# Two graph attention layers on one core: the norm's sums on ScalarE, the own-row product as a bf16 map, the scores of layer 1 after the second gather, and a new order of the start

## The chip, the cores and the metric

The kernel runs on one core of one Trainium2 chip. The metric is the device time of one execution in microseconds, as a median over runs. A profile of one further execution gives every instruction's start and length. PE is TensorE, DVE is VectorE, ACT is ScalarE, POOL is GpSimd, and SP issues the DMAs.

## The reference, cut to what matters

```python
# x: (16, 1024, 64) f32; adj: (16, 1024, 1024) int32, about 9 ones in a row, symmetric, ones on the diagonal
# layer 0: 8 heads of 64, edge kinds adj
q, k, v = x @ Wq + bq, x @ Wk + bk, x @ Wv + bv            # each reshaped to 8 heads
scores  = leaky_relu(q k^T / 8 + edge_bias[adj], 0.2)      # where adj > 0, else -1e9
x = layernorm(x + softmax(scores) v @ Wp + bp)             # over the 64 features, eps 1e-5
# layer 1: additive attention
hp = x @ lin_w^T + lin_b
u, v = hp @ W1^T, hp @ W2^T
e = sum_f a_f * leaky_relu(u_i + v_j, 0.2)                 # where adj > 0, else -9e15
x = layernorm(x + elu(softmax(e) hp))
```

## The kernel before, in words

The kernel uses the few ones of a row. Of each batch it first makes short lists of neighbours: groups of 8 rows share a list of columns. Those lists select rows of x (as one-hot matrices), and both attentions run over 120 slots per group instead of 1024 columns. A path over all pairs exists behind a flag and isn't taken with these inputs.

**Setup.** Weights are loaded and folded on PE and DVE (`aqk`, `wvp`, `wc8`, `lin2`, `w1h`, `w2d`), in tile pools that are closed before the pools of the main part open. `wc8` holds the same 512 numbers in a pattern with zeros; it is written in 128 copies of one column (L121).

**Lists of a batch** (`prepare`, `finish`). 16 pieces of adj (`ad`, 256 KB each, four buffers) are loaded; DVE turns each into 0 or a small number in bf16 (`ab`, L325, one buffer for half a batch); PE sums them with a code (`pat`, L334); DVE takes the best 40 of each segment with MAX8 and MATCH_REPLACE8 (L345 to L380), and writes the columns (`col`) and the row codes (`slot`) to DRAM, from where `cb` and `rows_s` come back copied over partitions. `prepare` is a generator of 41 pieces. Batch 0 is prepared whole at the start; a later batch is prepared in pieces, at five *places* in each step of the main loop (`lists.place(g, 0)` to `(g, 4)`), at most two pieces at a place. Small jobs (`side`) are advanced one piece at each place too.

**Main loop.** The order on every engine is the program's order, written out by hand. Step g works on tile g of layer 0 (eight tiles of 128 rows to a batch, so 128 in all) and on tile u = g - 12 of layer 1; the parts of a tile are spread over several steps. A step's main parts in their order on PE, with the lines of the profile:

- layer 0 `score` (L626), `gather` (L504, two halves), `heads` (L694), `rows`, `queries` (L605);
- layer 1 `project` of the tile before: `pz` takes the neighbours' product (L760) and the own row's product (L766). For the latter `own_rows` makes `ub`, the row of u repeated in 8 copies of which a mask leaves one (POOL, L748), and `rw`, a row of slots (ACT, L753);
- place 1; layer 1 `gather` first half (L504), `turn_weights` (L800, and its copy `eT` by DVE, L802); layer 0 `turn` (L523); place 2;
- layer 1 `weigh`, the scores from r (L786), and their maximum m (DVE, L788); `exps` (ACT, L794); layer 0 `indicate` (DVE, L480, two instructions); layer 1 `gather` second half;
- layer 0 `turn_weights` (L668, copies `w` by ACT, L670), layer 1 `turn`; place 3; layer 1 `indicate` (L480) and `own_rows`; layer 0 `attend` (z, L678), layer 1 `attend` (L811); place 4.

Between `project` and `weigh` stands r: ACT takes the positive part (L771) and DVE adds the rest (L772). The PSUM tag "e" has one bank; it is used in turn for `back`, for the transposed weights (L800, read by `eT`) and for the scores of `weigh`.

The norm (`Norm`) takes two tiles at once: DVE makes mean and variance with bn_stats and bn_aggr (L550, L551); POOL adds eps, takes the power -0.5 (L559), subtracts and multiplies (L558 to L563). Layer 0 does this in `residual`, layer 1 in `end`.

Of the kernel before, what the change touches and what calls it, by code (L numbers as in the profile page):

```python
# [22 lines left out]
GR = 8  # L23
# [10 lines left out]
def kernel(  # L34
# [18 lines left out]
    fst = fast.enter_context(tc.tile_pool(name="fst", bufs=1))  # L53
    setup = ExitStack()
    ps_c = setup.enter_context(tc.tile_pool(name="ps_c", bufs=4, space=bass.MemoryType.PSUM))
    tmp = setup.enter_context(tc.tile_pool(name="tmp", bufs=1))
    ident = cst.tile([P, P], F32, name="ident")
# [4 lines left out]
    nc.gpsimd.memset(ones, 1.0)  # L62


    def sub(n):
        return slice(n * D, n * D + D)

    def load_w(w, name, rows_, cols_):
        t = tmp.tile([rows_, cols_], F32, tag=name, name=name)
        nc.sync.dma_start(t, w)  # L70
        return t
# [14 lines left out]
    def head_T(w, name):  # L86
        t = tmp.tile([P, NC, D], F32, tag=name, name=name)
        for c in range(NC):
            pw = bank(f"{name}_{c}")
            nc.tensor.transpose(pw[:, 0, 0:D], w[:, ts(c, P)], ident[0:D, 0:D])  # L90
            nc.vector.tensor_copy(t[:, c, :], pw[:, 0, 0:D])
        return t
# [12 lines left out]
    qb = fst.tile([P, H], F32, name="qb")  # L105
    wc8 = halves("wc8", [GR, H, GR])
    wc1 = tmp.tile([1, H], F32, name="wc1")
    for h in range(H):
        c, r = h // 2, sub(h % 2)
        pw = bank(f"h_{h}")  # L110
        pc = bank(f"hc_{h}")
        for n in range(2):
            o = sub(n)
            nc.tensor.matmul(pw[o, 0, 0:D], wqT[r, c, :], wkT[r, c, :], start=True, stop=True)
            nc.tensor.matmul(pw[o, 1, 0:D], wvT[r, c, :], wp_l[r, c, :], start=True, stop=True)
            nc.tensor.matmul(pw[o, 2, 0:1], wkT[r, c, :], bq_c[r, c : c + 1], start=True, stop=True)
            nc.tensor.matmul(pw[o, 3, 0:1], wqT[r, c, :], bk_c[r, c : c + 1], start=True, stop=True)
            nc.vector.tensor_scalar(aqk[o, h, :], pw[o, 0, 0:D], QS1, None, ALU.mult)
            nc.vector.tensor_copy(wvp[o, h, :], pw[o, 1, 0:D])
            for i in range(GR):  # L120
                nc.vector.tensor_scalar(wc8[o, i, h, i : i + 1], pw[o, 3, 0:1], QS1, None, ALU.mult)  # L121
        nc.vector.tensor_scalar(qb[:, h : h + 1], pw[:, 2, 0:1], QS1, None, ALU.mult)
        nc.tensor.matmul(pc[0:1, 0, 0:1], bq_c[r, c : c + 1], bk_c[r, c : c + 1], start=True, stop=True)
        nc.vector.tensor_scalar(wc1[:, h : h + 1], pc[0:1, 0, 0:1], QS1, None, ALU.mult)
    eb1 = tmp.tile([1, H], F32, name="eb1")
    nc.sync.dma_start(eb1, edge_bias[1:2, :])
# [108 lines left out]
    nc.gpsimd.iota(jrow, [[-P, SEG // P]], base=SEG, channel_multiplier=-1, allow_small_or_imprecise_dtypes=True)  # L235

    bad = cst.tile([P, 1], F32, name="bad")
    nc.vector.memset(bad, 0.0)
# [19 lines left out]

    per = fast.enter_context(tc.tile_pool(name="g_per", bufs=1))
    dbl = fast.enter_context(tc.tile_pool(name="g_dbl", bufs=2))  # L260
    sml = fast.enter_context(tc.tile_pool(name="g_sml", bufs=4))
    ps_g = fast.enter_context(tc.tile_pool(name="ps_g", bufs=2, space=bass.MemoryType.PSUM))
    ps_s = fast.enter_context(tc.tile_pool(name="ps_s0", bufs=2, space=bass.MemoryType.PSUM))
    ps_p = fast.enter_context(tc.tile_pool(name="ps_p", bufs=2, space=bass.MemoryType.PSUM))
    ps_z = fast.enter_context(tc.tile_pool(name="ps_z", bufs=1, space=bass.MemoryType.PSUM))

# [42 lines left out]
    def prepare(b):  # L309
# [10 lines left out]
        for hs in range(2):  # L320
            ab = per.tile([P, NT, 2, SEG], BF16, tag="ab", name=f"ab_{b}_{hs}")
            for T in range(NT):
                ad = ads.pop(hs * NT + T)

                nc.vector.tensor_scalar(ab[:, T, :, :], ad, 1.0 - TINY, 0.0, ALU.subtract, ALU.max)  # L325
                if T % 4 // 2 == hs:
# [69 lines left out]
        for n in range(2):  # L396
            for s in range(NSEG):
                nc.sync.dma_start(col_d[:, s, n], col[sub(n), s, :])
        yield
        hv = who.rearrange("p (s a) k -> p s a k", a=2)  # L400
# [12 lines left out]
        for n in range(2):  # L413
            for q in range(NQ):
# [5 lines left out]
                )  # L420
        edges[b] = col_d
        late[b] = (flags, dg, rows_s)
# [22 lines left out]

    def thirds(src, tag, nm):

        t3 = dbl.tile([P, 3, NT, D], BF16, tag=tag, bufs=3, name=f"{tag}_{nm}")
        less = per.tile([P, NT, D], F32, tag="less", name=f"less_{tag}_{nm}")
# [91 lines left out]
    class Norm:  # L541
# [5 lines left out]

        def look(self, y, t):
            s6 = sml.tile([P, 6], F32, tag="st", name=f"st_{self.nm}_{t}")
            nc.vector.bn_stats(s6, y[:, t, :])  # L550
            nc.vector.bn_aggr(self.mv[:, t, :], s6)  # L551

        def scale(self, dst, y, t):
            two = slice(t - 1, t + 1)
            for t_ in (t - 1, t):
                self.look(y, t_)
            rs = sml.tile([P, 2], F32, tag="rs", name=f"rs_{self.nm}_{t}")
            nc.gpsimd.tensor_tensor(rs, self.mv[:, two, 1], eps.to_broadcast([P, 2]), ALU.add)  # L558
            nc.gpsimd.tensor_tensor(rs, rs, root.to_broadcast([P, 2]), ALU.pow)  # L559
            nc.gpsimd.tensor_tensor(  # L560
                dst[:, two, :], y[:, two, :], self.mv[:, two, 0:1].to_broadcast([P, 2, D]), ALU.subtract
            )
            nc.gpsimd.tensor_tensor(  # L563
                dst[:, two, :], dst[:, two, :], rs.unsqueeze(2).to_broadcast([P, 2, D]), ALU.mult
            )

    class Layer0(Tiles):
# [145 lines left out]
        def residual(self, t):  # L713
            if t % 2 == 0:
                return
            nc.vector.tensor_tensor(self.y[:, t - 1 : t + 1, :], self.pr, self.xs[:, t - 1 : t + 1, :], ALU.add)
            self.norm.scale(self.y, self.y, t)

# [8 lines left out]
    class Layer1(Tiles):  # L727
# [9 lines left out]
        def sums(self):  # L737
# [4 lines left out]
            self.u = dbl.tile([P, NT, D], F32, tag="u", bufs=1, name=f"u_{self.b}")  # L742
            nc.vector.tensor_tensor(self.u, pu, rows_b[:, 0:1, :].to_broadcast([P, NT, D]), ALU.add)

        def own_rows(self, t):
            nm = f"{self.b}_{t}"
            ub = dbl.tile([P, NQ, D], F32, tag="ub", name=f"ub_{nm}")
            nc.gpsimd.tensor_tensor(  # L748
                ub, self.u[:, t, :].unsqueeze(1).to_broadcast([P, NQ, D]), in_q.unsqueeze(2).to_broadcast([P, NQ, D]),
                ALU.mult,  # L750
            )
            rw = dbl.tile([P, SLOTS], F32, tag="rw", name=f"rw_{nm}")
            nc.scalar.activation(rw, masks[self.b][:, t, :], AF.Identity, bias=ones[:, 0:1], scale=-1.0 / NEG)  # L753
            self.rows_[t] = ub, rw

        def project(self, t):
            xg, (ub, rw) = self.xg[t], self.rows_.pop(t)
            pz = banks("s", f"pz_{self.b}_{t}")
            for n, c_ in CORNERS:
# [3 lines left out]
                )  # L763
            for p in range(4):
                for n, c_ in CORNERS:
                    nc.tensor.matmul(  # L766
                        pz[n][sub(c_), p, :], ub[sub(n), 2 * p + c_, :], rw[sub(n), :], start=False, stop=(p == 3)
                    )
# [28 lines left out]
        def turn_weights(self, t):  # L797
# [3 lines left out]
            eT = dbl.tile([SLOTS, P], F32, tag="eT", name=f"eT_{nm}")  # L801
            nc.vector.tensor_copy(eT, pt)  # L802
            self.e[t] = eT
# [25 lines left out]
        def end(self):  # L829
# [13 lines left out]
            for t in range(1, NT, 2):  # L843
                norm.scale(o, y, t)
                yield
                yield
# [17 lines left out]
    class Lists:  # L864


        def __init__(self):
# [5 lines left out]
            self.work = parts()  # L873
            self.done, self.part, self.side = 0, None, []

        def place(self, g, k):
# [3 lines left out]
            end = self.done + 2 if (t, k) != (NT - 1, PLACES - 1) else due  # L880
            while self.done < min(due, end) and self.part != ("keys" if last else "sums"):
                self.part = next(self.work, None)
                self.done += 1
            while self.side:
                if next(self.side[0], 0) is None:
                    break
                self.side.pop(0)

    order = ["PE", "Activation", "DVE", "Pool", "SP"]
    lists = Lists()  # L890
    with tc.manual_schedule(engines={getattr(mybir.EngineType, e) for e in order}):
        for _ in prepare(0):
            pass
        for _ in finish(0):
            pass
        l0[0] = Layer0(0)
        for _ in lists.side.pop():
            pass
        l0[0].constants()
        l0[0].load(0)  # L900
        l0[0].load(1)
        l0[0].indicate(0)
        l0[0].own(0)
        for g in range(NT * B + LAG + 7):
            u = g - LAG
# [27 lines left out]
            lists.place(g, 2)  # L933
            at(l1, u - 1, "weigh")
            at(l1, u - 1, "exps")
            at(l0, g + 1, "indicate")
            at(l0, g + 2, "load")
            at(l1, u, "gather", 1)
            if t == 2 and b - 1 in l0:
                x1 = l0[b - 1].end()  # L940
# [438 lines left out]
```

## Time and profile before

| | |
|---|---|
| median of 3 runs | 2493.3 us (2490.24 to 2495.37) |
| profiled execution | 2495.43 us, its span 2493.5 us |
| granted clock of TensorE | 0.98 of full speed on the mean; 0.83 in the first 200 us, 1.00 from 300 us on |
| busy: PE, DVE, ACT, POOL | 91%, 78%, 59%, 41% |
| first gather on PE | at 95.25 us |
| one batch in the steady state | 145.63 us (1138.70 to 1284.33) |

The span is from the first instruction to the last. A row of groups shows the line, the engine, the operation, tiles written and read, the count, the busy time in all and the mean length of one. A row of waits reads "who <- for whom: us in total, times, longest". A row of a timeline shows start, length, and in brackets the idle time of the engine just before and who ended it.

### The profile page before, as it was taken

The page shows a single profiled execution, that of the slowest core. Times are in us where ns is not written, and L with a number is a line of the kernel's source. Part 1 is how long each engine was busy: PE and PEld are TensorE (multiplying, and loading weights), DVE is VectorE, ACT ScalarE, POOL GpSimd, SP SyncE. Part 2 cuts the span into 40 slices and gives each one's busy share as a digit, 9 for nine tenths or more (in the row PEclk, how much of TensorE's full clock was granted, in tenths as well). Part 3 has the DMA queues.
Part 4 walks back from the last instruction along what each step waited for, and adds up shares of the span by engine and source line. Part 5 has one row for each costly group of instructions (what it writes and reads, how often), then busy time and mean ns, then how long its engine had stood idle before and what let it go on. Part 6 is the DMA issues. An engine that isn't in the chain of part 4 may idle for free.

```text
span 2493.5 us, 112320 instructions
## 1 busy us (share of the span) xinstructions
PE 2260.5 (91%) x49218; PEld 1910.4 (77%) x49218; DVE 1943.8 (78%) x5365; ACT 1459.4 (59%) x4417; POOL 1017.8 (41%) x1489
## 2 busy tenths in 40 slices
PE   5377899999999999999999999999999999999996
PEld 4266788888787887878788787878878787888864
DVE  6586878888887888788788878878887887876542
ACT  0054566666565665656566565656666665666743
POOL 1033433535354453534445353444535344443431
PEclk9688999999999999999999999999999999999998
DMA  3313242333233242323324332332423233132211
GB/s 103 96 56 119 79 146 78 108 113 119 81 97 124 78 129 92 122 78 92 129 78 127 93 121 78 96 124 78 142 85 116 78 117 104 57 100 67 70 38 29
DMA packets 192710, 239.10 MB, mean 96 GB/s; under 512 B 91732, under 2 KB 157332, under 8 KB 192212
## 3 DMA queue, kind: packets, MB, share of 16 engines
q1 hardware_dynamic: 192212, 231.85, 29.9%
q8 instruction: 388, 6.36, 1.0%
q14 instruction: 110, 0.90, 0.1%
HBM read 226.58 MB, written 5.21 MB: 93 GB/s over the span
## 4 chain that ended last, share of the span: by engine, by line
PE 62%; DVE 30%; DMA 3%; issue 3%; ACT 1%; POOL 1%; SPq 0%; POOLq 0%; ACTq 0%; DVEq 0%
PE pg L504 20%; PE pt L523 5%; PE s L626 5%; DVE r L772 4%; PE z L678 4%; PE pp L668 4%; PE pa L811 4%; PE po L694 3%; DMA ad<-in_adj_dram 3%; DVE f L480 3%; PE e L786 3%; PE pq L605 3%; DVE qp L610 2%; PE pat L334 2%; PE pz L766 2%
## 5 line engine op out<-in xcount | busy, mean ns | idle before, releaser
L504 PE MATMUL pg<-f,x 128*64 128x272 bf16 (+2 forms) x13312 | 807.1, 273 | 37.3 <-DVE f L480 33.7
L504 PEld LDWEIGHTS <-x 128*64 128x64 bf16 x13312 | 662.4, 110 | 117.5 <-issue 71.9
L660 POOL TENSOR_TENSOR ls<-ls,den 128x480 f32<-128x480 f32 x256 | 298.5, 1166 | 595.9 <-DVE den L659 593.1
L510 ACT COPY xg<-pg 128x448 f32<-128x448 f32 x512 | 271.6, 530 | 388.2 <-PE pg L504 386.3
L480 DVE TENSOR_SCALAR f<-cb,jrow 128x2176 bf16<-128x2176 bf16 x512 | 411.4, 847 | 0.1
L652 ACT ACTIVATE ls<-ls,mx 128x120 f32<-128x120 f32 x1024 | 391.3, 386 | 0.0
L524 ACT COPY xn<-pt 120x512 f32<-120x512 f32 x512 | 278.2, 598 | 43.6 <-PE pt L523 41.8
L523 PE MATMUL pt<-ident,xg 128*120 128x128 f32 x2048 | 271.6, 275 | 15.7 <-DVE qp L610 15.2
L523 PEld LDWEIGHTS pt<-ident,xg 128*120 128x120 f32 x2048 | 230.7, 138 | 23.7 <-DVE qp L610 16.7
L771 ACT ACTIVATE r<-pz 128x480 f32<-128x480 f32 x256 | 132.1, 568 | 174.5 <-PE pz L766 174.5
L489 POOL COPY xg<-xT 128x64 f32<-128x64 f32 x256 | 107.9, 432 | 291.3 <-PE pt L523 291.3
L634 DVE TENSOR_TENSOR sc<-s,rowc 128x480 f32<-128x480 f32 x256 | 155.5, 649 | 84.6 <-PE s L626 82.7
L772 DVE SCALAR_TENSOR_TENSOR r<-pz,r 128x480 f32<-128x480 f32 x256 | 155.6, 649 | 54.3 <-ACT r L771 53.2
L652 ACT ACTIVATION_READ_ACCUMULATOR ls<-ls,mx 128x1 f32 x1024 | 194.7, 190 | 0.0
L558 POOL TENSOR_TENSOR rs<-mv,eps 128x2 f32<-128x2 f32 x128 | 32.3, 253 | 359.2 <-DVE den L659 280.6
L642 DVE SCALAR_TENSOR_TENSOR ls<-sc 128x480 f32<-128x480 f32 x256 | 175.5, 686 | 0.0
L643 DVE TENSOR_REDUCE mx<-ls 128x4 f32<-128x480 f32 x256 | 167.2, 653 | 8.8
L766 PEld LDWEIGHTS pz<-rw,ub 64*64 64x64 f32 x4096 | 121.3, 133 | 62.7 <-issue 61.3
L678 PE MATMUL z<-w,xn 120*64 120x64 f32 x4096 | 158.7, 228 | 4.8 <-ACT w L670 4.1
L678 PEld LDWEIGHTS z<-w,xn 120*64 120x64 f32 x4096 | 137.6, 140 | 28.6 <-ACT w L670 26.3
L610 DVE TENSOR_TENSOR qp<-pq,qb 128x256 f32<-128x256 f32 x256 | 96.2, 418 | 78.9 <-PE pq L605 78.5
L748 POOL TENSOR_TENSOR ub<-u,in_q 128x512 f32<-128x512 f32 x128 | 155.4, 1215 | 0.1
(216 smaller groups left out, 4169.1 us busy)
## 6 DMA issues: line engine op xcount, KB each, us to landing
cb<-col_d SPq DMA_DIRECT2D x271, 544.0 KB
ad<-in_adj_dram SPq DMA_DIRECT2D x256, 256.0 KB
xs<-in_x_dram SPq DMA_DIRECT2D x32, 128.0 KB
rows_s<-slot_d SPq DMA_DIRECT2D x256, 14.0 KB
out_dram<-o SPq DMA_DIRECT2D x32, 128.0 KB
col_d<-col SPq DMA_DIRECT2D x128, 4.2 KB
dg<-in_adj_dram SPq DMA_DIRECT2D x32, 2.0 KB
slot_d<-slot SPq DMA_DIRECT2D x16, 28.0 KB
```

Of the source, the lines that this page charges most:

```text
L480: nc.vector.tensor_scalar(fj.rearrange("p s n q k -> p (s n q k)"), cb.rearrange("p s n q k -> p (s n q k)"), jrow[:, j : j + 1], None, AL ...
L504: nc.tensor.matmul(pg[sub(n), :, FIRST * a_ + lo : FIRST * a_ + to], self.t3[:, k, 4 * hs + 2 * a_ + j, :], f[j][:, 2 * hs + a_, n, :, lo:to],
L510: nc.scalar.copy(dst, pg)
L523: nc.tensor.transpose(pt[:, q, :], xg[:, 4 * m + q, :], ident)
L524: nc.scalar.copy(self.xn[t][:, ts(m, 4), :], pt)
L642: nc.vector.scalar_tensor_tensor(ls, scs[n], SLOPE, scs[n], ALU.mult, ALU.max)
L643: nc.vector.tensor_reduce(self.mx[:, n, ts_], ls, XX, ALU.max, negate=True)
L652: nc.scalar.activation(ls[:, q, :], ls[:, q, :], AF.Exp, bias=neg[:, q : q + 1], accum_out=den[:, q : q + 1])
L660: nc.gpsimd.tensor_tensor(ls, ls, den.unsqueeze(2).to_broadcast([P, 4, SLOTS]), ALU.mult)
L678: nc.tensor.matmul(zz[sub(n), q, :], xn[:, q, sub(n)], w_[n][:, q // 2, sub(q % 2)], start=True, stop=True)
L766: nc.tensor.matmul(pz[n][sub(c_), p, :], ub[sub(n), 2 * p + c_, :], rw[sub(n), :], start=False, stop=(p == 3))
L772: nc.vector.scalar_tensor_tensor(r, pz[n], SLOPE / (1.0 - SLOPE), r, ALU.mult, ALU.add)
```

## The change

- **Own row's product as a map.** `sums` splits u into three bf16 parts (`thirds`, on POOL, one piece at a place). `own_rows` makes `rw` in bf16 and from it `rq`, the row of slots in 8 copies of which a mask leaves one (POOL, 960 elements for 512 of `ub`). `project` takes 3 x 4 products of 64x64 by 480 columns in bf16 where it took 4 x 4 of 64x64 by 120 columns in f32.
- **Moved scores.** `weigh` and `exps` of layer 1 come after the second half of the gather, and so after `indicate` of layer 0 on DVE.
- **Norm.** Two ACTIVATEs with a row sum give the two means (Identity), POOL subtracts; at the next place two more (Square) give the variances, and POOL does the rest. `Norm.scale` is a generator; layer 0 puts it into a list of its own that is advanced at each place.
- **A copy.** `eT` is made by ACT.
- **Start.** The pools of the main part are opened before those of setup; `wc8` is made by one product; batch 0's `ab` is made by ACT; the first `cb` loads, `constants` and Layer0 come ahead of the row codes' loads and of `finish(0)`; at g = 0 no piece of a list is made.

```diff
@@ setup
-    wc8 = halves("wc8", [GR, H, GR])
+    wc8 = fst.tile([P, GR, H, GR], F32, name="wc8")
...
-            for i in range(GR):
-                nc.vector.tensor_scalar(wc8[o, i, h, i : i + 1], pw[o, 3, 0:1], QS1, None, ALU.mult)
+        nc.vector.tensor_scalar(wcv[:, h : h + 1], pw[:, 3, 0:1], QS1, None, ALU.mult)
...
+    nc.vector.tensor_tensor(
+        wc8, wcv.unsqueeze(1).unsqueeze(3).to_broadcast([P, GR, H, GR]),
+        same.unsqueeze(2).to_broadcast([P, GR, H, GR]), ALU.mult,
+    )
@@ prepare
-                nc.vector.tensor_scalar(ab[:, T, :, :], ad, 1.0 - TINY, 0.0, ALU.subtract, ALU.max)
+                if b:
+                    nc.vector.tensor_scalar(ab[:, T, :, :], ad, 1.0 - TINY, 0.0, ALU.subtract, ALU.max)
+                else:
+                    nc.scalar.activation(ab[:, T, :, :], ad, AF.Relu, bias=below)
...
+        edges[b] = col_d
         yield
@@ Norm
         def scale(self, dst, y, t):
-            for t_ in (t - 1, t):
-                self.look(y, t_)
...
+            for t_ in (t - 1, t):
+                nc.scalar.activation(
+                    part, y[:, t_, :], AF.Identity, scale=1.0 / D, accum_out=self.mv[:, t_, 0:1]
+                )
             nc.gpsimd.tensor_tensor(
                 dst[:, two, :], y[:, two, :], self.mv[:, two, 0:1].to_broadcast([P, 2, D]), ALU.subtract
             )
+            yield
+            for t_ in (t - 1, t):
+                nc.scalar.activation(
+                    part, dst[:, t_, :], AF.Square, scale=1.0 / D**0.5, accum_out=self.mv[:, t_, 1:2]
+                )
...
@@ Layer0.residual
-            self.norm.scale(self.y, self.y, t)
+            lists.norms.append(self.norm.scale(self.y, self.y, t))
@@ Layer1
+            self.u3, parts = thirds(self.u, "u3", f"{self.b}", 2)
+            lists.side.insert(0, parts)
...
-            ub = dbl.tile([P, NQ, D], F32, tag="ub", name=f"ub_{nm}")
...
+            rw = dbl.tile([P, SLOTS], BF16, tag="rw", name=f"rw_{nm}")
+            nc.scalar.activation(rw, masks[self.b][:, t, :], AF.Identity, bias=ones[:, 0:1], scale=-1.0 / NEG)
+            self.rows_[t] = rq = dbl.tile([P, NQ, SLOTS], BF16, tag="rq", name=f"rq_{nm}")
+            nc.gpsimd.tensor_tensor(
+                rq, rw.unsqueeze(1).to_broadcast([P, NQ, SLOTS]), in_q.unsqueeze(2).to_broadcast([P, NQ, SLOTS]), ALU.mult
+            )
...
-            for p in range(4):
+            for k in range(3):
                 for n, c_ in CORNERS:
                     nc.tensor.matmul(
-                        pz[n][sub(c_), p, :], ub[sub(n), 2 * p + c_, :], rw[sub(n), :], start=False, stop=(p == 3)
+                        pz[n][sub(c_), :, :], self.u3[sub(n), k, t, :],
+                        rq[sub(n), :, :].rearrange("p (g c) k -> p c g k", c=2)[:, c_, :, :], start=False, stop=(k == 2),
                     )
...
-            nc.vector.tensor_copy(eT, pt)
+            nc.scalar.copy(eT, pt)
@@ place
-            while self.done < min(due, end) and self.part != ("keys" if last else "sums"):
+            while g > 0 and self.done < min(due, end) and self.part != ("keys" if last else "sums"):
...
-            while self.side:
-                if next(self.side[0], 0) is None:
-                    break
-                self.side.pop(0)
+            for queue in (self.side, self.norms):
+                while queue:
+                    if next(queue[0], 0) is None:
+                        break
+                    queue.pop(0)
@@ main loop
-            at(l1, u - 1, "weigh")
-            at(l1, u - 1, "exps")
             at(l0, g + 1, "indicate")
             at(l0, g + 2, "load")
             at(l1, u, "gather", 1)
+            at(l1, u - 1, "weigh")
+            at(l1, u - 1, "exps")
```

## The prediction

> **What bounds the kernel now.** I read the busy shares first, then PE's waits, then one period of the steady state step by step, then its timeline, and last the chain before the first gather.
>
> ```profile
> PE 2260.5 (91%) x49218; PEld 1910.4 (77%) x49218; DVE 1943.8 (78%) x5365; ACT 1459.4 (59%) x4417; POOL 1017.8 (41%) x1489
> ```
>
> PE is the busiest, but 91% is a mean over a start of 95 us before the first gather and a thin end. PE's waits between 300 and 2200 us:
>
> ```profile
> PE e L786 <- DVE eT L802: 75.5, 76, 1.5
> PE pt L800 <- DVE den L659: 7.0, 20, 0.5
> ```
>
> So in the steady state PE is paced by its own order but for one wait: `weigh` (L786) writes the bank that `eT` (L802) must have left, and DVE comes late to that copy. Over the run it is 83.4 us. One batch, cut at the end of each L766 group, has eight steps of 145.63 us in all. The busy time by stretches gives the last two of them and the sums:
>
> ```profile
> 1247.44:1265.14 17.70, 16.17 (x372) 14.17 (x373) 16.79 (x58) 11.12 (x34) 5.93 (x10) 1.00 0.19 66
> 1265.14:1284.33 19.19, 17.83 (x412) 15.39 (x413) 17.79 (x46) 11.49 (x35) 8.55 (x9) 1.00 0.45 130
> sum 145.63, PE 137.64 PEld 117.17 DVE 120.29 ACT 90.81 POOL 63.91; mean PE 17.21 PEld 14.65 DVE 15.04 ACT 11.35 POOL 7.99
> ```
>
> Columns after the length: PE, PEld, DVE, ACT, POOL. In these two steps DVE idles only 0.91 and 1.40 us: there DVE sets the pace, in the other six PE does. PE's timeline of one step:
>
> ```profile
> 1207.74 0.99 PE L760 MATMUL pz<-xg,w2d 64*64 64x480 f32 x8
> 1208.55 1.00 PE L766 MATMUL pz<-rw,ub 64*64 64x120 f32 x32
> 1209.48 1.59 PE L504 MATMUL pg<-f,x 128*64 128x272 bf16 x26
> 1211.16 1.04 PE L523 MATMUL pt<-ident,xg 128*120 128x128 f32 x8
> 1213.72 0.62 PE L786 MATMUL e<-r,a_two 128*32 128x120 f32 x16 [1.53 <-DVE eT L802]
> 1214.32 1.59 PE L504 MATMUL pg<-f,x 128*64 128x272 bf16 x26
> 1217.79 1.48 PE L678 MATMUL z<-w,xn 120*64 120x64 f32 x31
> ```
>
> **The product with u (L766).** From its start to the next group's it takes 1209.48 - 1208.55 = 0.93 us. In its place come 12 bf16 products of 64x64 by 480 columns. The rate: L504's 26 products of 272 columns take 1.52 us, two column halves beside each other, so 0.117 us a pair or 0.43 ns a column; 480 columns are 0.206 us. L760 has four corners beside each other (8 records of 567 ns within 0.81 us). Four at a time, 12 products are 3 rounds, 0.62 us: a gain of 0.31 us. Two at a time it would be 1.24 us, a loss of 0.31. I take four at a time, because L760 is the same shape. 128 x 0.31 = 40 us of PE; in the two DVE-paced steps of eight it does not arrive, so 30 us (ends: +40 and -40).
>
> **weigh after the second gather, and eT on ACT.** Call P the end of the product with u. Today DVE does r (to P+1.87), then the work of two places, and eT in the middle of it; that is the 1.53 us. In the new order weigh stands behind 1.52 us more of PE work, and eT stands in ACT's queue behind one xg copy, about P+2.6. The wait on L786 goes. What is late next: `exps` now stands in ACT directly ahead of the two w copies, and waits for the maximum m (L788), which in DVE now stands behind both L480 of the next tile:
>
> ```profile
> 1215.99 0.25 DVE L788 TENSOR_REDUCE m<-e 128x1 f32<-128x120 f32 x1
> 1216.16 1.47 DVE L480 TENSOR_SCALAR f<-cb,jrow 128x2176 bf16<-128x2176 bf16 x2
> ```
>
> z (L678) needs both w. From m's start to the end of the second w is 0.28 + 0.05 + 0.45 + 1.08 = 1.86 us (DVE row, hop, exp with its read, two L670 copies). PE's own order gives z at P + 1.52 + 0.16 + 0.95 + 1.52 + 0.67 + 0.95 + 0.95, about P+6.66 (first gather, L800, L523, second gather, weigh, L668, L523). So z waits where m starts later than P+4.8. m's place is r's end, plus both places' DVE work, plus 1.42 for the L480 pair. In the step above (P = 1209.55) r ends at P+1.87, the two places hold 2.0 and, without bn_stats, 1.55 us of lists and mask work, and 1.42 follow: P+6.9. Read so from DVE's timeline, the eight steps of the period give P+5.2, 4.2, 4.2, 4.0, 6.9, 5.2, 7.1, 6.2, with bn_stats and eT taken out. Old z is weigh's end today (between P+3.25 and P+4.84) plus 1.52 + 0.95 + 0.95. New z against old z: gains of 0.07, 0, 0, 0.9, -0.5, 0.97, -0.7, 0.07 us, or 0.8 a batch of the 5.8 that are waited today. With 14.5 batches of both layers: 12 us, not 83. Ends: 83 if DVE catches up, and a loss of 60 if m is later everywhere by as much as in its worst step (2.3 us).
>
> **Norm on ACT.** DVE loses 256 x (208 + 182) ns = 100 us of busy rows, and eT 35.7 us; the places that pace it are steps 7 and 8, with one pair of tiles (0.77 us as it stands in DVE's timeline) and two eT (0.2 each): 1.2 us x 14.5 = 17 us. ACT gets 512 ACTIVATEs of 64 columns with a read. The row is L652: 120 columns, 386 ns, and a pitch of 0.38 us with its read (190 ns, overlapped); a 64-column copy (L816) is 212 ns. So 0.33 us each, 169 us, and 128 eT at 0.28 us, 36 us: ACT goes from 11.35 to 12.95 us a step, and does not become the bound. Layer 0's two halves stand behind both `r` activations and behind both xn copies, where ACT waits for PE today. Layer 1's first pair straddles a step: its squares stand ahead of `exps` and wait for a subtraction that POOL does behind rq; some 1.7 us once a batch, mostly in steps where DVE idles 4 us or more, so I count +5 us (0 to 25).
>
> **POOL.** rq has 960 elements where ub had 512. From L748 (1.04 us undisturbed for 512) and L660 (1.17 for 480) it is 2.0 to 2.3 us: +0.9 x 128 = 115 us, and u's thirds add 3 x 0.61 + 2 x 1.16 = 4.2 us a batch. POOL goes from 44% to about 55% of a step; rq now waits for rw on ACT, and what queues behind it, the next divide, needs later ACT work anyway. The cost lies in DVE: undisturbed L480 takes 0.777 us, beside a POOL instruction 0.896 on the mean and up to 1.8. I count 8 us (0 to 30).
>
> [...] The row of before shows 0.12 us a time, with shorter POOL instructions, and I go by the row.
>
> **Before the first gather.** In the chain from 0 to 97 us:
>
> ```profile
> 9.09 0.60 DVE wc L121 x8
> 37.83 4.30 DMA ad<-in_adj_dram
> 47.51 5.58 DMA ad<-in_adj_dram
> 83.05 1.53 DMA slot_d<-slot
> 90.16 4.13 DMA cb<-col_d
> ```
>
> The 128 small wc writes go (8.4 us of that chain by its shares, of which I count 6: PE's products follow at once). The conversion of batch 0 (`ab`) runs on ACT during setup, so the first 4.30 us load and the conversions around it are hidden (6 us more); the second stall stays in part, since `ab` has one buffer, but it now overlaps DVE's first lists (5 us). The 16 rows_s issues from 84.59 to 90.1 go behind cb (5.5 us). Sum 22 us (15 to 30). Work left out at g = 0 is made up within two steps: nothing.
>
> **The end.** Twelve steps of layer 1 alone, 9.45 us each today with pz, r, r, eT, e in one chain: now gathers lie beside r. About 0.7 us each, -8. The last norm goes from 1.8 us a pair to about 2.6: +3. Sum -5.
>
> **Sum**: -30 - 12 - 17 + 5 + 8 - 22 - 5 = -73 us on the profiled execution of 2495.43 (span 2493.5 and 1.9 outside): 2422. That execution lies 2.1 above the median of 2493.3, so 2420.
>
> **Rivals.** One: the old wait goes and nothing replaces it. For it: six of eight steps have DVE idle for 1.5 us or more. Against it: m behind the L480s. Then 83 in place of 12, 40 in place of 30, no DVE term, no 13 of cost: -40 - 83 - 22 - 5 = -150, so 2343. Two, slower: the wait of z for w, through m and exp, exceeds what it replaces. The gains beside it are 30 + 17 + 22 + 5 = 74, with 83 from the old wait 157; over 116 full steps the break-even is 1.35 us a step. My list averages 0.9, the worst two steps have over 2. If L480s held up by rq add 0.7 us to each step, z waits 1.6: 116 x 1.6 - 157 = +29, so 2522. Three: POOL and ACT eat most of the steady gain, and only the start and the u product in part remain: -30, 2463. That the squares would need another table on ACT is excluded: the built program has one table load, as before (one L532 load of 1.28 us).
>
> **Chances.** My forecast 0.50, rival one 0.20, three 0.13; slower 0.13; no change 0.04, where 0.2% (5 us) is about what a measurement can tell. Faster: 0.83. The range goes to just under rival one's time, 2338, and past three's to 2475; above it lie slower and no change, below it the better half of rival one.
>
> **What would show it.** L786 no longer waits for eT; a new PE row z <- ACT w of some 0.9 us a step, with m behind L480 in DVE; the u product at 0.62 us; the first gather near 73 us; rq near 2.1 us; one table load. It is wrong if z waits more than 1.35 us a step, if the 12 products take over 0.9 us, or if ACT rows start to hold PE's xg or pt.

## The result and the profile after

The changed kernel takes 2490.99 us (median of 12 runs), the kernel before 2494.27 us beside it: a ratio of 0.9979 (95% interval 0.9967 to 0.9991), 5 us where 73 had been forecast. Its profiled execution has a span of 2489.6 us. The engines' row of its page:

```profile
PE 2260.9 (91%) x46658; PEld 1870.6 (75%) x46658; DVE 1813.8 (73%) x4591; ACT 1613.4 (65%) x5585; POOL 1206.3 (48%) x1570
```

DVE lost 130 us of work and PE 2560 instructions, yet PE's busy time is what it was. PE's waits between 300 and 2200 us:

```profile
PE z L694 <- ACT w L686: 59.6, 104, 1.5
PE pt L818 <- DVE den L675: 18.7, 25, 1.2
PE pg L516 <- ACT xg L522: 12.5, 11, 1.2
```

The wait of `weigh` for `eT` (75.5 us) is gone and z waits for w, as foretold; but the other two rows grew too: all rows of PE's waits in this stretch add up to 100.1 us, in the kernel before to 92.7. One batch takes 146.19 us against 144.53 (mean over the 96 steps of r from tile 8 to tile 104). The gain is all at the start: the first gather comes at 80.2 us (95.25), r of layer 1's first tile ends at 271.9 us (295.6). From there to r of the last tile it takes 16 us longer, and the end another 3.8. One wait of z in the timeline:

```profile
1058.34 1.48 DVE L492 TENSOR_SCALAR f<-cb,jrow 128x2176 bf16<-128x2176 bf16 x2
1059.73 0.28 DVE L806 TENSOR_REDUCE m<-e 128x1 f32<-128x120 f32 x1
1060.40 1.06 ACT L686 COPY w<-pp 120x512 f32<-120x512 f32 x2
1061.03 0.33 PE L694 MATMUL z<-w,xn 120*64 120x64 f32 x2 [1.20 <-ACT w L686]
1063.47 1.75 PE L642 MATMUL s<-xg,qp 64*64 64x120 f32 x32
```

The chain is the forecast one: two one-hots, m, exp, w, z. The last line was not forecast: the 32 products of s take 1.75 us where they take 1.05 otherwise. The granted clock falls to 0.5 for 3.41 us, 17 times between 300 and 2200 us (58 us in all); before, it never falls there.

Two more stretches of the changed kernel show what the experiments below single out, POOL's rq. First DVE beside it:

```profile
1099.70 1.83 POOL L769 TENSOR_TENSOR rq<-rw,in_q 128x960 bf16<-128x960 bf16 x1 [2.90 <-ACT rw L767]
1099.91 1.66 DVE L376 TENSOR_TENSOR left<-left,left 128x32 int32<-128x32 int32 x1
1102.15 0.19 DVE L378 TENSOR_TENSOR left<-left,left 128x32 int32<-128x32 int32 x1
```

A DVE instruction on 32 columns takes 1.66 us and ends with rq; the same line takes 0.19 us in 50 of its 64 times. Then the norm of layer 1:

```profile
439.58 1.79 POOL L769 TENSOR_TENSOR rq<-rw,in_q 128x960 bf16<-128x960 bf16 x1
441.33 0.41 POOL L568 TENSOR_TENSOR o<-y,mv 128x128 f32<-128x128 f32 x1
441.76 0.26 ACT L573 ACTIVATE part<-o 128x64 f32<-128x64 f32 x1 [1.73 <-POOL o L568]
444.67 0.93 ACT L522 COPY xg<-pg 128x448 f32<-128x448 f32 x2
445.23 1.00 PE L516 MATMUL pg<-f,x 128*64 128x272 bf16 x16 [1.17 <-ACT xg L522]
```

ACT stands 1.73 us before the squares, because POOL's subtraction stands behind rq; the exps and the xg copy behind them come late, and PE's gather waits 1.17 us.

### The profile page after: what moved, and what is told of

Its sections match the earlier page's. It is cut to its first block, busy times and chain, and to the rows that moved or that the text cites. A ratio compares the mean times of both kernels' runs of the same rounds, so it can differ in the third digit from the quotient of the medians.

```text
span 2489.6 us, 107460 instructions
## 1 busy us (share of the span) xinstructions
PE 2260.9 (91%) x46658; PEld 1870.6 (75%) x46658; DVE 1813.8 (73%) x4591; ACT 1613.4 (65%) x5585; POOL 1206.3 (48%) x1570
## 5 line engine op out<-in xcount | busy, mean ns | idle before, releaser
L516 PEld LDWEIGHTS <-x 128*64 128x64 bf16 x13312 | 669.5, 110 | 154.0 <-issue 125.2
L492 DVE TENSOR_SCALAR f<-cb,jrow 128x2176 bf16<-128x2176 bf16 x512 | 432.4, 885 | 15.0 <-DMA cb<-col_d 15.0
L769 POOL TENSOR_TENSOR rq<-rw,in_q 128x960 bf16<-128x960 bf16 x128 | 229.9, 1796 | 114.8 <-ACT rw L767 114.8
L535 PEld LDWEIGHTS pt<-ident,xg 128*120 128x120 f32 x2048 | 230.7, 138 | 27.9 <-DVE qp L626 18.7
L694 PE MATMUL z<-w,xn 120*64 120x64 f32 x4096 | 173.2, 227 | 65.9 <-ACT w L686 65.8
L694 PEld LDWEIGHTS z<-w,xn 120*64 120x64 f32 x4096 | 146.6, 138 | 99.4 <-ACT w L686 93.9
L658 DVE SCALAR_TENSOR_TENSOR ls<-sc 128x480 f32<-128x480 f32 x256 | 181.3, 708 | 0.0
L642 PE MATMUL s<-xg,qp 64*64 64x120 f32 x4096 | 148.0, 286 | 4.1 <-DVE qp L626 3.4
L829 PE MATMUL pa<-eT,xn 120*64 120x8 f32 x4096 | 145.7, 202 | 4.8 <-ACT xn L536 3.9
```

What stands on the lines that cost most here:

```text
L492: nc.vector.tensor_scalar(fj.rearrange("p s n q k -> p (s n q k)"), cb.rearrange("p s n q k -> p (s n q k)"), jrow[:, j : j + 1], None, AL ...
L516: nc.tensor.matmul(pg[sub(n), :, FIRST * a_ + lo : FIRST * a_ + to], self.t3[:, k, 4 * hs + 2 * a_ + j, :], f[j][:, 2 * hs + a_, n, :, lo:to],
L535: nc.tensor.transpose(pt[:, q, :], xg[:, 4 * m + q, :], ident)
L642: nc.tensor.matmul(both[n][sub(c_), p, :], w.rearrange("p h i -> p (h i)"), src, start=(k + p == 0), stop=(k + p == 4),)
L658: nc.vector.scalar_tensor_tensor(ls, scs[n], SLOPE, scs[n], ALU.mult, ALU.max)
L694: nc.tensor.matmul(zz[sub(n), q, :], xn[:, q, sub(n)], w_[n][:, q // 2, sub(q % 2)], start=True, stop=True)
```

## The experiments

Theory one: DVE's chain to m, and the clock behind z's wait, took the gain. Theory two: work put on ACT and POOL took it, rq above all. Each kernel was timed in three rounds against the kernel before on the same chip. "Us" is (ratio - 1) x 2493, so that runs on different chips compare; an interval is 3 to 9 us to each side, so differences of a few us say little.

| run | ratio (95%) | us | a batch, us |
|---|---|---|---|
| the change | 0.9979 (0.9967, 0.9991) | -5 | 146.19 |
| b5_start_alone | 0.9944 (0.9928, 0.9960) | -14 | 144.55 |
| b1_eT_alone | 0.9988 (0.9976, 1.0000) | -3 | 143.30 |
| b4_norm_alone | 0.9985 (0.9970, 1.0000) | -4 | 144.76 |
| b3_map_alone | 1.0035 (1.0018, 1.0052) | +9 | 144.77 |
| b2_moved_alone | 1.0162 (1.0127, 1.0197) | +40 | 147.57 |
| a1_scores_back | 1.0055 (1.0036, 1.0074) | +14 | 146.85 |
| a2_m_first | 1.0065 (1.0045, 1.0086) | +16 | 147.01 |
| a3_fill_wait | 0.9951 (0.9932, 0.9970) | -12 | 144.95 |
| a6_map_back | 0.9986 (0.9975, 0.9997) | -3 | 145.85 |
| c1_start_eT | 0.9930 (0.9905, 0.9955) | -17 | 143.73 |
| c2_start_eT_norm | 0.9937 (0.9912, 0.9963) | -16 | 144.17 |
| c3_map_back_fill | 0.9935 (0.9913, 0.9957) | -16 | 144.97 |
| d1_rq_once | 0.9830 (0.9805, 0.9855) | -42 | 142.16 |
| d2_scores_back_rq_once | 0.9726 (0.9700, 0.9752) | -68 | 140.50 |
| d3_pool_load | 1.0185 (1.0160, 1.0210) | +46 | 147.25 |
| e1_half_rq | 0.9932 (0.9915, 0.9948) | -17 | 144.10 |
| e2_half_rq_dve | 0.9840 (0.9823, 0.9856) | -40 | 142.31 |
| e4_half_rq_moved | 0.9980 (0.9964, 0.9996) | -5 | 145.58 |

### The order of the scores, and the clock

a1 puts `weigh` and `exps` back ahead of `indicate`; a2 leaves them behind the gather and takes `indicate` behind them:

```diff
 # a1
+            at(l1, u - 1, "weigh")
+            at(l1, u - 1, "exps")
             at(l0, g + 1, "indicate")
...
             at(l1, u, "gather", 1)
-            at(l1, u - 1, "weigh")
-            at(l1, u - 1, "exps")
 # a2
-            at(l0, g + 1, "indicate")
-            at(l0, g + 2, "load")
             at(l1, u, "gather", 1)
             at(l1, u - 1, "weigh")
             at(l1, u - 1, "exps")
+            at(l0, g + 1, "indicate")
+            at(l0, g + 2, "load")
```

> The changed kernel with weigh and exps of layer 1 back ahead of indicate and of the second gather, all else kept. Theory one (the chain r, lists, m, exp, w copies, z sets the steady state, and PE's wait for w lets the granted clock drop to 0.5 for 3.4 us): PE's wait of z for w falls from 4.6 us a batch to about 2.5 (m no longer behind the two one-hot instructions), the clock drops go for the most part (26 of them, 45 us), 2491 becomes about 2420. Theory two (the work put on ACT and POOL ate the gain): 2491 within 10, clock as before it.

> The changed kernel with PE's order as it is, and only indicate of layer 0 put behind weigh and exps, so that DVE makes the maximum m ahead of the two one-hot instructions. Theory one: the wait of z for w falls from 4.6 us a batch to about 1.5, no or few clock drops, about 2400. Theory two: 2491 within 10.

Both lost: a1 is 19 us slower than the change, a2 21 us. z no longer waits in a1 (6.1 us in a2), but PE waits for DVE elsewhere. The waits of a1 between 300 and 2200 us:

```profile
PE pt L818 <- DVE den L675: 29.2, 35, 1.2
PE po L710 <- DVE sc L650: 28.1, 13, 2.2
PE e L804 <- ACT eT L820: 19.1, 13, 1.5
```

DVE has the same instructions as in the change and is busy 1870.8 us in place of 1813.8; its one-hots (L492) take 939 ns on the mean, in the change 885. So the late m was no matter of order alone: something stretches DVE, and it depends on what lies beside it. The timeline of a1 shows what:

```profile
674.58 3.01 DVE L492 TENSOR_SCALAR f<-cb,jrow 128x2176 bf16<-128x2176 bf16 x2
674.86 2.14 POOL L769 TENSOR_TENSOR rq<-rw,in_q 128x960 bf16<-128x960 bf16 x1 [0.85 <-ACT rw L767]
```

Two one-hots take 3.01 us in place of 1.48. The first starts before rq and takes 0.78 us; the second starts 0.42 us after rq's start and takes 2.31 us. In a1, 26 one-hots start within an rq: each of them takes 2.31 or 2.32 us and ends 0.58 us after rq's end.

a3 fills z's wait in three steps of eight with products of constants, whose sums are overwritten:

```diff
             zz = ps_z.tile([P, NQ, D], F32, tag="z", name=f"z_{self.b}_{t}")
+            if (t + 2) % NT in (0, 2, 3) and NT * self.b + t > 12:
+                for _ in range(5):
+                    nc.tensor.matmul(zz..., ident_b, rep_q..., start=True, stop=True)
```

> The changed kernel with five bf16 products of 128x128 by 512 columns (1.1 us) put on PE ahead of z in the three steps of eight where z waits 1.3 to 1.6 us; their sums are overwritten by z. Theory one, second half: z starts when it did, but the clock no longer drops: 45 us less, about 2446. If the recorded drops cost nothing, or come from something else than the idle wait: 2491 within 10.

No fall of the clock is left between 300 and 2200 us, and the kernel is 7 us faster than the change, with 195 recorded products of 379 ns more on PE in that stretch. The clock's falls do cost, but far less than expected: 7 us of measured gain, beside an estimated 29 us that 58 us at half speed would cost if PE had nothing to wait for. PE's waits in a3:

```profile
PE pt L824 <- DVE den L675: 22.2, 31, 1.2
PE z L700 <- ACT w L686: 15.6, 77, 0.4
```

Part of what PE wins it spends on waits for DVE. Theory one holds as a mechanism and is too small.

### The parts alone, on the kernel before

b1: the copy `eT` by ACT. b2: the moved scores. b3: the map product (`sums`, `thirds`, `own_rows`, `project`). b4: the norm (`Norm`, the list of norms). b5: the start, with all else as before. Each is that part of the diff shown above, in `before`; b1 and b2 whole:

```diff
 # b1
-            nc.vector.tensor_copy(eT, pt)
+            nc.scalar.copy(eT, pt)
 # b2
-            at(l1, u - 1, "weigh")
-            at(l1, u - 1, "exps")
             at(l0, g + 1, "indicate")
...
             at(l1, u, "gather", 1)
+            at(l1, u - 1, "weigh")
+            at(l1, u - 1, "exps")
```

> The kernel before with the copy eT on ACT, nothing else. If the copy itself was what PE waited for: the wait of 83 us goes and about 2410 is left. Theory one (DVE's lists between r and m set the step, and the wait only shows where that chain meets PE): the wait of weigh for eT goes, but DVE comes late elsewhere (z for w, po for sc), and 2440 to 2490 is left.

> The kernel before with the moved scores alone. Theory one: the wait of weigh for eT goes, z waits for w in its place, with bn_stats still on DVE some 6 to 8 us a batch, and clock drops come: slower than before by 20 to 70 us. Theory two: faster than before by up to 80 us.

> The kernel before with the own row's product as a bf16 map, nothing else. PE alone: 0.21 us a tile as the changed kernel's profile has it, 27 us less, 2467. Theory two (POOL's longer rq, 1.8 us for 1.2, and u's thirds hold DVE's one-hot instructions): these get slower than 847 ns on the mean, DVE gets later, and the time stays at 2494 or rises.

> The kernel before with the norm's sums on ACT in two passes, nothing else. Theory one: DVE has 100 us less in the chain that paces it, eT comes earlier, PE's wait for it falls: 2450 to 2480. Theory two: ACT's squares wait for POOL, ACT's copies come late, and nothing is gained: 2494 within 10.

> The kernel before with the new start alone (pools, wc8, ab of batch 0 on ACT, order of the first loads, no list piece at g = 0). Both theories: the first gather near 80 us for 95, 15 to 24 us less in all, 2472 to 2480, the steady state as before.

Only the start is worth something alone. The sum of the parts is +28 us, the whole -5: the parts act on each other. eT on ACT takes the wait of e from 75.5 to 11.9 us, and 27.9 us of pt <- xg and 13.8 of po <- sc take its place. The norm takes 100 us off DVE and PE does not notice. The moved scores alone bring 18 falls of the clock (109 us at half speed). The map, with 0.21 us less PE a tile, is slower: its one-hots take 920 ns in place of 847, and e <- eT rises from 75.5 to 84.5 us.

### The map taken back, and the parts put together

```diff
 # a6: the change with `sums`, `thirds`, `own_rows` and `project` of before
 # c1: the kernel before with the start and eT on ACT
 # c2: c1 and the norm on ACT (= a1 without the map)
 # c3: a6 with a3's products ahead of z
```

> The changed kernel with the row-map product of layer 1 as before it (own map expanded as ub by POOL, float32 product by the fp32 row flags); moved scores, norm on ACT, eT on ACT and the start stay. Theory one (the move of the scores and the clock behind its waits ate the gain; the map product is worth its 0.21 us a tile): the u product back costs 1.7 us a batch, the z waits and the drops stay: about 27 us slower than the changed kernel, 2518 us. Theory two (POOL's rq and the thirds of u hold DVE's one-hots, and with that everything behind them): the one-hots go from 0.885 us back to about 0.83, m and w come earlier, the z waits fall from 165 us to under 60 and the drops from 17 to under 6; the map back costs 27 us, its cover gives 40 or more: 2475 us or below.

> The kernel before with the two parts that won alone and are off POOL: the start (0.9944) and eT on ACT (0.9988). Both theories: the parts lie in different stages, so they add: 2494 - 14 - 4 = 2476 us; by the batch of eT alone (143.3 against 144.5 us, 14 batches) it would be 2463 us. No clock drops between 300 and 2200 us.

> The kernel before with start, eT on ACT and the norm on ACT (everything of the change but the moved scores and the map product). Theory one (DVE's load sets the waits): the norm takes 4.5 us a batch of statistics off DVE, which has 15 us less wait for e: 2470 us or below. Theory two (what goes to ACT comes back as waits for ACT's copies): ACT's eT and the norm's squares meet in front of the xg copy, pt L535<-ACT over 40 us: no faster than start and eT alone, 2476 us or above.

> The changed kernel with the map product as before and five products of constants ahead of z in three steps of eight (their sums are overwritten), so no clock drops. Theory one: 27 us over the changed kernel with the fill, 2510 us. Theory two: below the changed kernel with the fill, 2470 us or less; if the map back alone already has no drops, the fill costs its own 0.6 us a step and is slower than without it.

c1 is the sum of its parts (-17). The norm adds nothing to it (c2). The map costs 30 us on top of c2 (a1), but nothing where the scores are moved (a6 against the change): with moved scores no one-hot is held by rq (14 touch one, each at 0.78 us). Conversely the moved scores cost 12 us without the map (a6 against c2) and win 19 with it (the change against a1). a6 fits neither theory: it is neither 27 us slower nor 16 faster. PE's waits in a6:

```profile
PE z L694 <- ACT w L686: 47.3, 92, 1.5
PE pt L816 <- DVE den L675: 8.7, 11, 1.2
PE pg L516 <- ACT xg L522: 0.8, 4, 0.2
```

All rows add up to 74 us, in the change to 100.1: with the map PE waits 26 us more, and the rows of z, den and xg alone grow by 34. That is about what its shorter product saves (27 us). The clock falls 9 times in a6, 17 times in the change. c3, with the same filling as a3, is 13 us faster than a6 and has one fall left.

### rq by itself

d1 is the change, d2 is a1, both with POOL's product once a batch, for the first tile. The other seven tiles use the first one's row flags, so their sums are not those of the reference: d1 and d2 show times only. ACT's rw, PE's twelve products and u's thirds stay. d3 is the kernel before with rq as a dead product beside `ub`.

```diff
 # d1, d2
-            self.rows_[t] = rq = dbl.tile([P, NQ, SLOTS], BF16, tag="rq", name=f"rq_{nm}")
-            nc.gpsimd.tensor_tensor(rq, ...)
+            if t == 0:
+                self.rq = dbl.tile([P, NQ, SLOTS], BF16, tag="rq", name=f"rq_{nm}")
+                nc.gpsimd.tensor_tensor(self.rq, ...)
+            self.rows_[t] = self.rq
 # d3
             self.rows_[t] = ub, rw
+            rq = dbl.tile([P, NQ, SLOTS], BF16, tag="rq", name=f"rq_{nm}")
+            nc.gpsimd.tensor_tensor(rq, ...)
```

> The changed kernel with rq multiplied by POOL once a batch, for its first tile, and used for all eight (the row flags of tiles 1 to 7 are those of tile 0, so these sums are wrong); ACT still makes rw for every tile, PE's 12 products and u's thirds stay. It takes 112 of the 128 rq, some 200 us, off POOL. If POOL's rq is what the map product costs (it holds DVE's one-hots): L492 falls from 0.885 to about 0.84 us, the waits of pt, pg and z shrink, and the map's 1.7 us of PE a batch arrives: 2491 - 27 = 2464 us or below. If the map's cost lies elsewhere (u's thirds, the product's own length, the clock): L492 falls or not, and the time stays within 8 us of 2491.

> The same with the scores at their old place (start, norm, eT and map; rq once a batch). Start, norm and eT with the old product gave 2477 us, with the map 2509 us: 32 us for the map. If POOL's rq is the cause, all 32 us come back and the product's 27 us besides: 2450 us, L492 at 0.85 us, the waits po<-sc and pt<-den at 13 and 18 us as with the old product. If the cause is elsewhere in the map: 2500 us or above.

> The kernel before with one multiplication of rq's size more on POOL a tile, whose result nobody reads; ub and PE's products stay. POOL gets 128 x about 1.9 us = 240 us, 2.1 times what the change adds to it by rq. If POOL's load holds DVE's one-hots and this reaches PE: L480 rises from 0.847 to 0.95 us or more, and the time by 30 us or more, 2525 us. If POOL's load is harmless in itself: within 8 us of 2494.

So rq's time on POOL costs much more than forecast. 112 of POOL's 128 rq taken away are worth 37 us in the order of the change and 82 us in the old one; rq added to the kernel before costs 46 us. d1 and d2 have no `ub` either, which the kernel before pays for, so 37 and 82 us are prices against no product of POOL at all. What rq adds to `ub` can only be estimated, from the 27 us of PE work that the map saves (0.21 us a tile): some 25 us in the order of the change (a6 against the change), 57 in the old order (c2 against a1), 36 alone (b3). DVE's busy time falls from 1870.8 to 1795.3 us from a1 to d2, with the same instructions. The waits of d2 between 300 and 2200 us:

```profile
PE e L806 <- ACT eT L822: 19.1, 13, 1.5
PE pt L820 <- DVE den L675: 14.8, 23, 0.8
PE po L710 <- DVE sc L650: 6.0, 12, 0.6
```

Against a1 the two waits for DVE are 37 us shorter, and a1's seven falls of the clock are gone. In d1, pg <- xg no longer appears among the first waits and the clock's falls are 6 in place of 17.

For DVE's instructions that start within an rq, what each takes above its undisturbed length (the 5th percentile of its line and operation, worked out from the trace) adds up to 79 us in a1, 28 in the change, 70 in b3, 83 in d3. For `ub` it is already 36 us in the kernel before, 30 in c2 and 26 in a6: in the order of the change rq holds DVE hardly more than `ub` did. In d3 the one-hots, with a mean of 0.86 us, bear little of it; there a cast of 44 columns takes 1.77 us and ends with rq:

```profile
305.28 1.82 POOL L756 TENSOR_TENSOR rq<-rw,in_q 128x960 bf16<-128x960 f32 x1
305.37 1.77 DVE L404 CAST slot<-who 128x44 bf16<-128x44 int32 x1
```

So L492's mean alone, which the expectation of d3 took as the sign, is the wrong sign; which DVE instruction is held depends on the order. A rival to these holds is that rq makes POOL's other work late. In d3 it does not: between 300 and 2200 us DVE has no row of waits for POOL and ACT one of 0.8 us, and the waits that PE gains there are for DVE (pz <- sc 8.6 us, den 11.3 in place of 7.0, po <- sc 3.2, eT 78.6 in place of 75.5).

Gaps of PE are not all of it. Of the 6.4 us a batch between a1 and d2, 3.8 are idle time of PE. The other 2.6 us are longer records: `po`, behind whose waits the clock falls in a1, and the first products of `pz` (L777), which take over 1.4 us in 21 of 104 tiles of a1 and in one of 109 of d2, where 0.99 is usual (26 of 103 in d3, 6 of 105 in the kernel before). Why `pz` takes longer is not shown.

### Versions with a shorter rq

Each half of the eight groups lies in one half of the rows. e1 keeps u's thirds twice, masked to one half of the rows each, so that rq needs four copies instead of eight (480 elements); PE runs 24 products of 240 columns. The scores are at their old place. e2 makes this rq on DVE, e4 is e1 in the order of the change.

```diff
+            self.u2 = dbl.tile([P, 2, 3, NT, D], BF16, tag="u2", bufs=1, name=f"u2_{self.b}")
...
+                    nc.vector.tensor_scalar(self.u2[:, f], self.u2[:, 0], in_f[:, f : f + 1], None, ALU.mult)
...
+            self.rows_[t] = rq = dbl.tile([P, NQ // 2, SLOTS], BF16, tag="rq", name=f"rq_{nm}")
+            nc.vector.tensor_tensor(   # e2; e1 and e4: nc.gpsimd
+                rq, rw.unsqueeze(1).to_broadcast([P, NQ // 2, SLOTS]), in_4, ALU.mult
...
+                for f in range(2):
+                    for n, c_ in CORNERS:
+                        nc.tensor.matmul(
+                            pz[n][sub(c_), 2 * f : 2 * f + 2, :], self.u2[sub(n), f, k, t, :], ...
```

> A version: scores at their old place, start, norm, eT and the map, but with rq of four groups of slots in place of eight (480 elements): u's thirds are kept twice, once for each half of the groups, masked by DVE once a batch (about 1 us a batch), and PE runs 24 products of 240 columns in place of 12 of 480. POOL's rq should fall from 1.86 to about 1.05 us, half of what d2 took away. If POOL's time is the price, half of d2's gain comes: between 2509 us (rq whole) and 2423 us (rq once a batch), 2466 us, below every version so far. If the 24 products are slower than the 12 (more than 0.72 us a tile) or DVE's masks hurt, 2480 us or above.

> The same with the half rq made by DVE (bf16, constants of full length): POOL makes no rq at all, DVE gets 128 times some 0.35 to 0.55 us. If it is POOL's time in itself that counts, and DVE has room for it: near d2, 2435 us. If DVE is the pacing engine (its one-hots late, not slow): no better than e1, 2466 us or above.

> The changed kernel (scores moved) with the half rq on POOL: between 2491 us (whole) and 2446 us (once a batch): 2468 us; the z waits and the clock drops stay, so it is not faster than e1. If the moved scores still help where rq is long, it is under e1.

e1 hits: rq takes 1.06 us on POOL, and 31 of the 82 us come. 25 one-hots start within an rq, and each takes 1.51 us, again to 0.58 us behind rq's end: the price goes by rq's length. e4 gains nothing beside the change; z's wait (54.9 us) and seven falls of the clock stay. e2 computes the whole function and is the fastest version that does, 2450.96 us, 40 us under the kernel before. Its page, its rq in the groups view, and its waits:

```profile
PE 2243.0 (92%) x48194; PEld 1879.5 (77%) x48194; DVE 1859.4 (76%) x4754; ACT 1622.7 (66%) x5585; POOL 973.0 (40%) x1442
```

```profile
L786 DVE TENSOR_TENSOR rq<-rw,in 128x480 bf16<-128x480 bf16 x128 | 63.5, 496 | 92.9 <-ACT rw L784 91.2
```

```profile
PE e L822 <- ACT eT L838: 19.0, 13, 1.5
PE pt L543 <- ACT xg L530: 15.0, 34, 0.6
PE pt L836 <- DVE den L683: 11.7, 19, 0.8
```

DVE is given 63.5 us of rq and 19.7 us of masks, and ends with less busy time than in a1 (1859.4 against 1870.8): its other instructions are 95 us shorter in all.

## Why the prediction was wrong

Of the 73 us that were forecast 68 are missing. The step that weighs most is POOL's price (17 to 49 us of it, by the order of the parts); then come the norm (17), the end (9), the start (8) and the clock (7). The parts act on each other, so these misses don't add up exactly.

- **POOL, 8 us (0 to 30).** This step failed. rq's length was near (1.80 us on the mean in the change, forecast 2.0 to 2.3); its price was not. Against no product of POOL it measured 37 us in the order of the change and 82 us in the old order. What it adds to `ub`, which is what the term stood for, is estimated above at 25, 57 and 36 us: in the order of the change still within the stated 0 to 30, so there the term explains 17 us of the miss, in the old order 49. The mechanism was wrong in both: certain DVE instructions that start within rq last to its end or beyond, and the price goes by how many do, not by a mean. The mean of 0.12 us a time came from L480 beside all of POOL's instructions; 204 of those 316 keep 0.77 or 0.78 us. The second path, layer 1's squares on ACT behind POOL's subtraction behind rq, was seen, at +5 us (0 to 25); PE's wait for xg measured 12.5 us in 1900, in a6 0.8.
- **The hold.** In a1 and e1 51 one-hots start within an rq; each ends 0.58 or 0.59 us behind it, where its own length is 0.78. Others are not held: the 39 MAX8 and 36 `sc` that start within an rq in the change keep their 0.44 and 0.65 us. Single rows of the kernel before show the hold too. There L366 takes 0.19 us in 50 of its 64 times, and some 0.91 in the 13 that start within `ub`:

```profile
1256.00 1.05 POOL L748 TENSOR_TENSOR ub<-u,in_q 128x512 f32<-128x512 f32 x1
1256.19 0.91 DVE L366 TENSOR_TENSOR left<-left,left 128x32 int32<-128x32 int32 x1
```

- **The clock.** The sum had no term for it. Between 300 and 2200 us, 17 falls make 58 us of half speed; filling the waits is worth 7 us on the end in a3, and 13 in c3 against a6.
- **z's wait.** Right in place and chain, and its size was near: 4.6 us a batch against 7 forecast. But the waits beside it (den, xg) had been left out. Two sums of this step are off: PE's own order adds up to P+6.72, not 6.66, and the lower end, a loss of 60, does not follow from its worst step (116 waits of 2.3 us are 267 us, 184 more than the 83 that go). Neither decides the miss.
- **DVE's relief by the norm, 17 us.** Not there: alone -4 us with a batch no shorter, and +2 on top of start and eT. PE's wait for eT did fall in b4 (75.5 to 59.5 us), while den and others grew; why no batch became shorter is not shown.
- **The product with u.** 0.72 us from its start to the next group's (median), not 0.62: 0.21 us a tile and 27 us, not 40 (30 in the sum). That it reaches the end where rq is not in the way fits d1 (39 us under a6, of which `ub` has a share too).
- **The start, 22 us.** Short by a third: alone (b5) 14 us, with the first gather at 79.3 us, not 73, and the first r 11.7 us earlier. The 24 us at the first r of the change are not the start's alone: the norm alone brings 12.0 us there (b4), and its execution ends 5.3 us later behind the last r. In the change the end is 3.8 us longer where 5 us of gain stood.

Rival three, POOL and ACT eating most of the steady gain, was the right kind; it was given 13%, and its 2463 us still left too much over.

## What to carry to other kernels

Before you give an idle engine more work, look in the trace for single instructions of the engine that paces that end together with one of the idle engine (here L366, at 0.91 us for 0.19, with `ub`), not at means over a group. A piece of work whose own time is off the path can cost more than the work that it saves (here rq, an estimated 57 us above `ub` in the old order, for 27 us less on PE); ask whether the pacing engine can do it itself, in fewer elements. And price parts in the order in which they will stand: here the map cost 9 us alone, 30 in one order and nothing in another.

## What the runs showed of the hardware that was not expected

- Some DVE instructions that start within a POOL product are held to its end whatever their own size: 32 columns took 1.66 us (L376 of the change, 13 times, each to 0.05 us behind rq), 44 columns 1.77 us (d3), where such instructions take 0.17 to 0.19 us undisturbed; MAX8 (0.44 us) and `sc` (0.65 us) are not held. One-hots that start before rq keep their own length (14 of 14 in the change, 0.78 us).
- TensorE's granted clock fell to 0.5 for 3.41 us 17 times between 300 and 2200 us of the change, each time 2.1 to 2.7 us after the start of a z that had waited behind 16 transposes (`pp` and `pt`): 1.13 to 1.20 us in 16 of them, 1.48 us in one. Of the 38 waits of z of 1 us or more in that stretch 21 were followed by no fall, 12 of 1.47 to 1.49 us among them. In the kernel before, waits of up to 1.5 us (e <- eT, behind nine `pt` transposes) brought none; in a1, 7 of 13 waits of 2.16 us (po <- sc, behind the gather's products) did. The falls begin on a grid: from 329.80 to 384.42 us are 16 times 3.41 us, to 476.58 us 43 times. That filling the gap ends the falls is shown by a3: 17 in the change, none there. Why one wait is followed by a fall and another is not is not shown.
